# Pairing gate's last whole block with the block of the 64 last features, and seven block products in place of eight

## The chip, the cores and the metric

The kernel runs on one core of one Trainium2 chip. The metric is the device time of one execution in microseconds (us), lower is better. Times of single instructions come from the hardware profile of one execution.

## The reference

All arrays are float32. Only the second half of the computation, the feed-forward part, is touched by the change.

```python
# x: 2048 rows of 1024 values; F = 2752 features
x = x + layernorm(attention(layernorm(x)))
xt = layernorm(x)
up   = xt @ W_up.T            # W_up, W_gate: [2752, 1024]
gate = silu(xt @ W_gate.T)
y = gate * up @ W_down.T      # W_down: [1024, 2752]
out = x + layernorm(y)
```

The 2752 features are 21 whole blocks of 128 and one block of 64.

## The kernel before

**Precision.** A float32 operand is held as two rounded parts, high and low. One multiplication is then three matmuls (high by high, high by low, low by high), issued by `mmc` (lines 601 to 606). Splitting an operand is one ScalarE cast (line 108) and one VectorE subtraction (line 109).

**Halves and quadrants.** The feed-forward part goes over the 2048 rows in two halves, `s` = 0 and 1, of two groups of 512 rows each. Within a half, xt's transpose is seen as a 2 by 2 arrangement: B11 and B21 are the first and second 512 inputs of the first row group, B22 belongs to the second group. T1 to T4 are sums of these quadrants, built once a half.

**Products.** `prod(o, w, a, b)` multiplies a quadrant of 128 features by 512 inputs with one of B11, B21, B22, T1 to T4 of 512 inputs by 512 rows: four blocks of the inputs by three matmuls, 12 matmuls of 128x128 weights on 128x512 moving data, summed in one PSUM bank.

**Ten pairs.** For twenty of the feature blocks, block `p` and block `p + 10` are the two rows of a 2 by 2 quadrant matrix (class `Pair`, from line 493). The four quadrant results of such a matrix, which would take eight products, take seven: A11 by B11, A12 by B21, S1 by T1, S2 by T2, S3 by T3, A22 by T4, S4 by B22. S1 to S4 are sums of weight quadrants, made on VectorE by four operations of 128x512 (lines 528 to 531). `gate_up` (line 622) does this for gate and for up in turn, one product of gate and one of up, in the four banks `ag`, `au`, `cg`, `cu`.

**The rest.** What is left over is gate's block 20, up's block 20 and `wlast`, which holds the 64 last features of gate and the 64 last of up. Each is a `Single`: four products, A11 by B11 copied from bank `a` to SBUF and used again for the second row group, A11 by T1 and A12 by B22 in bank `c`, A12 by B21 added onto bank `a`. `gate_up_rest` (line 692) does the three of them, 12 products a half. Its results go to DRAM as `hr_d` (the whole block) and `hl_d` (the 64 features), each for row group 0 and 1.

**Down.** `run_down` follows with 78 steps a half, each a matmul of hidden features with W_down. It works in the other four banks.

**Buffers.** Weights pass through two rings. A load (512 KB from the SyncE queue) takes a raw buffer, of which there are four. A preparation (cast and subtraction, after the sums where there are some) takes one of six slots. A slot comes free when the last product that reads it is done (`done()`), and then the `Feeder` starts the next loads and preparations in a fixed order. A `Pair` takes two raw buffers and four slots, a `Single` and a step of down one raw buffer and one slot.

**Order.** Each engine's order is not the order of the text: a planner (`schedule_with_timeline_sim=True`) simulates the program when it is built. When an engine is free in that simulation, it gives it the instruction that is earliest in the text among those that are ready. So an engine that would wait is handed later work that is ready; the order so found is fixed in the kernel that runs. Where `keep_in_program_order` is used, the text's order holds.

Of the kernel before, what the change touches and what calls it, by code (L numbers as in the profile page):

```python
# [11 lines left out]
ALU = mybir.AluOpType  # L12
# [3 lines left out]
P = 128  # L16
# [10 lines left out]
FR = F - FB * P  # L27
NKB = T // P
EPS = 1e-5
NPAIR = 10  # L30
# [4 lines left out]
def block_kernel(ctx, tc, x, wqk, wv, bqk, bv, wo, bo, wgu, wlast, wd, out):  # L35
# [12 lines left out]
    nc = tc.nc  # L48
# [4 lines left out]
    def tl(p, shape, dt, name):  # L53
        return p.tile(shape, dt, tag=name, name=name, bufs=1)
# [32 lines left out]
    hl_d = [[tl(dram, [FR, 512], F32, f"hl_d{s}_{k}") for k in range(2)] for s in range(2)]  # L87
# [281 lines left out]
    def xq(name, cb):  # L369
        if name == "T2":  # L370
            return q2[cb // 2][:, cb % 2, :, :]
        t, c = XQ[name]
        return t[:, c + cb, :, :]
# [45 lines left out]
    class First:  # L419


        def __init__(self, dst, halves):
            self.dst, self.halves = dst, halves

        def load(self, r):
            self.r = r
            for h, d in zip((L, R), self.halves):
                nc.sync.dma_start(r[:, h], d)
# [58 lines left out]
    def w4(t):  # L487
        return t.rearrange("p (c h f) -> p c h f", h=2, f=P)
# [4 lines left out]
    class Pair:  # L493


        def __init__(self, p, m):
            self.p, self.m = p, m
            self.s = {}
            one, two_, three, four = Slot(), Slot(), Slot(), Slot()
            self.slot = [one, two_, three, four]  # L500

            self.at = {"A11": (one, 0), "A12": (one, 4), "S2": (two_, 0), "S1": (two_, 4), "S3": (three, 0), "S4": (three, 4), "A22": (four, 0)}
# [3 lines left out]

        def load(self):
            self.r = [raws.get(), raws.get()]
            for r, fb in zip(self.r, (self.p, self.p + NPAIR)):
                nc.sync.dma_start(r.rearrange("p (c f) -> p c f", f=P), wgu[fb, self.m])  # L510
            self.loaded = True

        loaded = False
# [87 lines left out]
    def mmc(o, w, m, first, last, chained, pin=lambda m: m):  # L601

        for n, (i, j) in enumerate(((0, 0), (0, 1), (1, 0))):
            one = nc.tensor.matmul(o, w[i], m[j], start=first and n == 0, stop=last and n == 2, skip_group_check=chained)  # L604
            if n == 0:
                pin(one)

    def prod(o, w, a, b, first=True):

        slot, c0 = w.at[a]  # L610
        v = w4(slot.need())
        for cb in range(4):
            x = xq(b, cb)
            mmc(o, (v[:, c0 + cb, 0, :], v[:, c0 + cb, 1, :]), (x[:, 0, :], x[:, 1, :]), first and cb == 0, cb == 3, not first)

    def add(o, a, b, op=ALU.add):
        nc.vector.tensor_tensor(o, a, b, op)  # L617

    def silu(o, a):
        nc.scalar.activation(o, a, AF.Silu)  # L620
# [68 lines left out]
        put("S2", u11)  # L689
        put("S4", g12)  # L690

    def gate_up_rest(s, wg, wu, wl, bg):
        ag, au, cg, cu = bg
        g11, g12, g22, g21, u11, u12, u22 = tmp[0:7]
        for w, a, c, u in ((wg, ag, cg, g12), (wu, au, cu, u12)):
            prod(a, w, "A11", "B11")
            nc.scalar.copy(u, a)
            prod(c, w, "A11", "T1")
        for w, a, c in ((wg, ag, cg), (wu, au, cu)):
            prod(a, w, "A12", "B21", False)  # L700
            prod(c, w, "A12", "B22", False)
            w.one.done()
        silu(g11, ag)
        add(g11, au, g11, ALU.mult)
        nc.sync.dma_start(hr_d[s][0], g11)
        add(g12, cg, g12)
        silu(g12, g12)
        add(u12, cu, u12)
        add(g12, g12, u12, ALU.mult)
        nc.sync.dma_start(hr_d[s][1], g12)  # L710
        prod(ag, wl, "A11", "B11")
        nc.scalar.copy(u11, ag)
        prod(cg, wl, "A11", "T1")
        prod(ag, wl, "A12", "B21", False)
        prod(cg, wl, "A12", "B22", False)
        wl.one.done()
        silu(g21[:FR, :], ag[:FR, :])
        add(g21[:FR, :], ag[FR : 2 * FR, :], g21[:FR, :], ALU.mult)
        nc.sync.dma_start(hl_d[s][0], g21[:FR, :])
        add(g22[:FR, :], cg[:FR, :], u11[:FR, :])  # L720
        silu(g22[:FR, :], g22[:FR, :])
        add(u22[:FR, :], cg[FR : 2 * FR, :], u11[FR : 2 * FR, :])
        add(g22[:FR, :], g22[:FR, :], u22[:FR, :], ALU.mult)
        nc.sync.dma_start(hl_d[s][1], g22[:FR, :])

    def load_down(p):
        for r, fb in zip(f4[0:2], (p, p + NPAIR)):
# [136 lines left out]
    X, Y = bank[0:4], bank[4:8]  # L864
    half = []
    for s in range(2):
        pairs = [(Pair(p, 0), Pair(p, 1)) for p in range(NPAIR)]
        rest = Single(wgu[2 * NPAIR, 0]), Single(wgu[2 * NPAIR, 1]), Single(wlast)
        dn = Down(s)
        half.append((pairs, rest, dn))  # L870
        for wg, wu in pairs:
            wg.queue_load()
            wu.queue_load()
            for i in range(4):
                wg.queue_prep(i)
                wu.queue_prep(i)
        for w in rest:
            w.queue_load()
            w.queue_prep(0)
        dn.queue()  # L880


# [85 lines left out]
    for s in range(2):  # L968
        pairs, rest, dn = half[s]
        bg, other = (X, Y) if s == 0 else (Y, X)  # L970
        for p in range(NPAIR):
            jobs = [] if s else [lambda: ahead(p), lambda: behind(p)]
            gate_up(s, p, *pairs[p], bg, jobs)
        gate_up_rest(s, *rest, bg)

        def next_x(cb):
            r1, r2 = raws2.get(), raws2.get()
            build_x(2, cb, r1, r2)
            raws2.free(r1)
            raws2.free(r2)  # L980

        if s == 0:
            run_down(s, dn, other, bg, 2 * TB * [None], [lambda cb=cb: next_x(cb) for cb in range(4)])
        else:
            xpool.release()
            x1pool = pool("x1", side="right")
            x1 = [tl(x1pool, [P, C], F32, f"x1_{k}") for k in range(2 * TB)]
            run_down(s, dn, other, bg, x1, [lambda k=k: nc.sync.dma_start(x1[k], x1_d[2 * TB + k]) for k in range(2 * TB)])
# [39 lines left out]
```

## Time and profile before

| | us |
|---|---|
| median of 3 runs | 1729.71 |
| lowest and highest | 1728.43 and 1729.87 |
| the profiled execution, its own time | 1728.61 |
| its span, first to last instruction | 1726.8 |
| TensorE busy | 1699.3 |
| VectorE busy | 1091.8 |
| ScalarE busy | 689.1 |

The granted TensorE clock was 0.992 of full in the mean. In the profile, PE is TensorE's matmuls, PEld its weight loads, DVE VectorE, ACT ScalarE, POOL GpSimd, SP SyncE. A group of instructions is written as line, engine, operation, output<-inputs by the program's names without their numbers: `xi` are the tiles for results (`g11`, `u12` and so on), `bank` the PSUM banks. A weight slot lies in `a` or in `wvo`; the quadrants of x are `xb` (B11, B21), `kx` (T1, T3), `qa` and `qb` (T2), `a` (T4, B22). So `bank<-xb,a` is a product with B11 or B21, `bank<-kx,a` one with T1 or T3, and `bank<-a` or `bank<-wvo` alone a step of down, whose two operands share a slot.

### The profile page before, as it was taken

The numbers are of one execution on the slowest core, as the hardware profiler recorded it, in microseconds if no ns is written. First come the engines' busy times: TensorE is split into PE (matmuls) and PEld (weight loads), VectorE is DVE, ScalarE is ACT, GpSimd is POOL, SyncE is SP. The second block draws the span as 40 slices with busy tenths as digits, with TensorE's granted clock in tenths as the row PEclk, the third lists the DMA queues.
The fourth block names the chain that finished last, engine by engine and source line by source line (L and its number), as shares of the span: only waits on it lengthen the run. The fifth ranks groups of instructions, "written<-read, shape, count | busy, mean of one in ns | idle before, by whom it ended". The sixth has DMA issues, their size and how long they took to land.

```text
span 1726.8 us, 21119 instructions
## 1 busy us (share of the span) xinstructions
PE 1699.3 (98%) x7788; PEld 1393.6 (81%) x7788; DVE 1091.8 (63%) x1666; ACT 689.1 (40%) x1031; POOL 89.0 (5%) x118
## 2 busy tenths in 40 slices
PE   8999999999899999999999999999999999999997
PEld 7888887888688888888888888788888888888886
DVE  8633667667877777676378457866555564345458
ACT  3222445544544444443355444433333333244343
POOL 1000001000011111110000000100000000000001
PEclk8999999999899999999999999999999999999999
DMA  6221023234755566665358655633332223486654
GB/s 210 80 80 37 37 74 125 97 126 172 257 195 195 201 215 214 214 204 190 122 191 255 194 194 193 205 105 113 129 109 94 91 92 122 132 280 195 195 185 159
DMA packets 131015, 271.01 MB, mean 157 GB/s; under 512 B 13280, under 2 KB 29792, under 8 KB 130912
## 3 DMA queue, kind: packets, MB, share of 16 engines
q1 hardware_dynamic: 128176, 262.72, 45.6%
q10 hardware_dynamic: 2736, 6.95, 1.1%
q8 instruction: 61, 1.00, 0.2%
q14 instruction: 42, 0.34, 0.1%
HBM read 185.73 MB, written 83.89 MB: 156 GB/s over the span
## 4 chain that ended last, share of the span: by engine, by line
PE 93%; DVE 3%; DMA 2%; issue 1%; ACT 1%; POOL 0%; SPq 0%; POOLq 0%; DVEq 0%; ACTq 0%
PE bank L604 70%; PE bank L146 4%; PE bank L145 4%; PE bank L147 4%; PE bank L275 3%; PE bank L276 2%; PE bank L267 1%; PE bank L205 1%; PE bank L206 1%; PE bank L346 1%; DMA f<-x 1%; PE bank L138 1%; DVE small L115 0%; PE bank L773 0%; PE bank L774 0%
## 5 line engine op out<-in xcount | busy, mean ns | idle before, releaser
L604 PE MATMUL bank<-a 128*128 128x512 f32 x1176 | 273.8, 390 | 0.0
L604 PEld LDWEIGHTS bank<-a 128*128 128x128 f32 x1176 | 220.8, 188 | 46.8
L604 PE MATMUL bank<-xb,a 128*128 128x512 f32 x816 | 197.3, 395 | 0.0
L109 DVE TENSOR_TENSOR a<-f2p,a 128x1024 fp32r<-128x1024 f32 (+2 forms) x114 | 124.7, 1095 | 93.4 <-ACT a L108 81.0
L617 DVE TENSOR_TENSOR xi<-bank,xi 128x512 f32<-128x512 f32 (+1 forms) x168 | 113.3, 685 | 111.1 <-PE bank L604 70.1
L604 PEld LDWEIGHTS bank<-xb,a 128*128 128x128 f32 x816 | 152.9, 187 | 37.1
L604 PE MATMUL bank<-kx,a 128*128 128x512 f32 x648 | 157.1, 395 | 0.0
L604 PE MATMUL bank<-a,a 128*128 128x512 f32 x648 | 153.4, 390 | 0.0
L108 ACT CAST a<-f2p 128x1024 fp32r<-128x1024 f32 (+2 forms) x114 | 107.6, 949 | 112.5 <-PE bank L604 102.4
L109 DVE TENSOR_TENSOR a<-f,a 128x512 fp32r<-128x512 f32 (+3 forms) x93 | 91.3, 981 | 91.4 <-ACT a L108 88.0
L604 PEld LDWEIGHTS bank<-kx,a 128*128 128x128 f32 x648 | 121.5, 187 | 29.5
L604 PEld LDWEIGHTS bank<-a,a 128*128 128x128 f32 x648 | 121.6, 188 | 26.4
L604 PE MATMUL bank<-wvo 128*128 128x512 f32 x600 | 142.4, 390 | 0.0
L604 PEld LDWEIGHTS bank<-wvo 128*128 128x128 f32 x600 | 112.6, 188 | 24.4
L108 ACT CAST a<-f 128x512 fp32r<-128x512 f32 (+3 forms) x93 | 69.4, 747 | 125.7 <-PE bank L604 90.6
L275 PE MATMUL bank<-a,a 128*128 128x512 f32 x256 | 94.5, 402 | 2.8 <-ACT f L348 2.0
L109 DVE TENSOR_TENSOR wvo<-f2p,wvo 128x1024 fp32r<-128x1024 f32 (+2 forms) x48 | 54.8, 1141 | 66.2 <-ACT wvo L108 57.6
L604 PE MATMUL bank<-a,wvo 128*128 128x512 f32 x384 | 93.7, 396 | 1.2 <-ACT xi L663 1.2
L604 PE MATMUL bank<-kx,wvo 128*128 128x512 f32 x384 | 91.9, 390 | 0.0
L617 DVE TENSOR_TENSOR xi<-xi,xi 128x512 f32<-128x512 f32 x124 | 85.4, 688 | 4.3
L604 PEld LDWEIGHTS bank<-a,wvo 128*128 128x128 f32 x384 | 72.0, 188 | 18.8 <-ACT xi L663 1.6
L604 PEld LDWEIGHTS bank<-kx,wvo 128*128 128x128 f32 x384 | 72.1, 188 | 15.7
(234 smaller groups left out, 2751.2 us busy)
## 6 DMA issues: line engine op xcount, KB each, us to landing
f2p<-wgu SPq DMA_DIRECT2D x43, 512.0 KB, 5.0
hd_S<-xi SPq DMA_DIRECT2D x80, 256.0 KB, 4.6
f<-x SPq DMA_DIRECT2D x30, 512.0 KB, 3.9
hd_A<-xi SPq DMA_DIRECT2D x60, 256.0 KB, 2.0
f<-wgu SPq DMA_DIRECT2D x21, 512.0 KB, 4.4
wr<-wgu SPq DMA_DIRECT2D x20, 512.0 KB, 5.9
f<-wd SPq DMA_DIRECT2D x20, 512.0 KB, 5.0
td_T<-f SPq DMA_DIRECT2D x40, 256.0 KB, 4.5
```

What stands on the lines that cost most here:

```text
L108: nc.scalar.copy(hi, src)
L109: (lo_engine or nc.vector).tensor_tensor(lo, src, f32(hi), ALU.subtract)
L138: nc.tensor.transpose(b[:, j * P : (j + 1) * P], t[:, cb * P : (cb + 1) * P], ident)
L145: nc.tensor.matmul(o, w[0], m[0], start=first, stop=False)
L146: nc.tensor.matmul(o, w[0], m[1], start=False, stop=False)
L147: nc.tensor.matmul(o, w[1], m[0], start=False, stop=last)
L205: nc.tensor.matmul(b, xg[:, c, 0, cols], wv_s[:, c, :, :].rearrange("p a f -> p (a f)"), start=(c == 0), stop=False)
L206: nc.tensor.matmul(b[:, D:], xg[:, c, 1, cols], wv_s[:, c, 0, :], start=False, stop=(c == 7))
L275: nc.tensor.matmul(b, p[:, k, 0, :], vt[:, k, :, :].rearrange("p h d -> p (h d)"), start=(k == 0), stop=False)
L276: nc.tensor.matmul(b[:, D:], p[:, k, 1, :], vt[:, k, 0, :], start=False, stop=(k == NKB - 1))
L604: one = nc.tensor.matmul(o, w[i], m[j], start=first and n == 0, stop=last and n == 2, skip_group_check=chained)
L617: nc.vector.tensor_tensor(o, a, b, op)
```

## The change

Gate's block 20 and `wlast` become the two rows of one `Pair`, with the seven products. Up's block 20 stays a `Single` with four. Its products are placed among the first eight. A half's `gate_up_rest` has 11 products where it had 12. The weights of the rest are prepared in the order: the pair's A11 and A12, up's, then the pair's S2 and S1, its S3 and S4, its A22. `Pair` takes its two sources as arguments.

```diff
-        def __init__(self, p, m):
-            self.p, self.m = p, m
+        def __init__(self, *src):
+            self.src = src
...
-            for r, fb in zip(self.r, (self.p, self.p + NPAIR)):
-                nc.sync.dma_start(r.rearrange("p (c f) -> p c f", f=P), wgu[fb, self.m])
+            for r, w in zip(self.r, self.src):
+                nc.sync.dma_start(r.rearrange("p (c f) -> p c f", f=P), w)
...
-    def gate_up_rest(s, wg, wu, wl, bg):
-        ag, au, cg, cu = bg
+    def gate_up_rest(s, wp, wu, bg):
+        ap, au, cp, cu = bg
         g11, g12, g22, g21, u11, u12, u22 = tmp[0:7]
-        for w, a, c, u in ((wg, ag, cg, g12), (wu, au, cu, u12)):
-            prod(a, w, "A11", "B11")
-            nc.scalar.copy(u, a)
-            prod(c, w, "A11", "T1")
-        for w, a, c in ((wg, ag, cg), (wu, au, cu)):
-            prod(a, w, "A12", "B21", False)
-            prod(c, w, "A12", "B22", False)
-            w.one.done()
-        silu(g11, ag)
+        prod(ap, wp, "A11", "B11")
+        nc.scalar.copy(g11, ap)
+        prod(au, wu, "A11", "B11")
+        nc.scalar.copy(u12, au)
+        prod(cp, wp, "A12", "B21")
+        wp.slot[0].done()
+        add(g11, cp, g11)
+        silu(g11, g11)
+        prod(cu, wu, "A11", "T1")
+        prod(ap, wp, "S2", "T2", False)
+        nc.scalar.copy(g12, ap)
+        prod(au, wu, "A12", "B21", False)
         add(g11, au, g11, ALU.mult)
         nc.sync.dma_start(hr_d[s][0], g11)
-        add(g12, cg, g12)
+        prod(cp, wp, "S1", "T1")
+        wp.slot[1].done()
+        prod(cu, wu, "A12", "B22", False)
+        wu.one.done()
+        add(u12, cu, u12)
+        prod(ap, wp, "S3", "T3", False)
+        nc.scalar.copy(g22, ap)
+        add(u22[:FR, :], cp[FR : 2 * FR, :], g22[FR : 2 * FR, :])
+        add(g22[:FR, :], cp[:FR, :], g22[:FR, :])
+        silu(g22[:FR, :], g22[:FR, :])
+        add(g22[:FR, :], g22[:FR, :], u22[:FR, :], ALU.mult)
+        nc.sync.dma_start(hl_d[s][1], g22[:FR, :])
+        prod(ap, wp, "A22", "T4", False)
+        wp.slot[3].done()
+        silu(g21[:FR, :], ap[:FR, :])
+        add(g21[:FR, :], ap[FR : 2 * FR, :], g21[:FR, :], ALU.mult)
+        nc.sync.dma_start(hl_d[s][0], g21[:FR, :])
+        prod(cp, wp, "S4", "B22", False)
+        wp.slot[2].done()
+        add(g12, cp, g12)
         silu(g12, g12)
-        add(u12, cu, u12)
         add(g12, g12, u12, ALU.mult)
         nc.sync.dma_start(hr_d[s][1], g12)
-        prod(ag, wl, "A11", "B11")
-        nc.scalar.copy(u11, ag)
-        prod(cg, wl, "A11", "T1")
-        prod(ag, wl, "A12", "B21", False)
-        prod(cg, wl, "A12", "B22", False)
-        wl.one.done()
-        silu(g21[:FR, :], ag[:FR, :])
-        add(g21[:FR, :], ag[FR : 2 * FR, :], g21[:FR, :], ALU.mult)
-        nc.sync.dma_start(hl_d[s][0], g21[:FR, :])
-        add(g22[:FR, :], cg[:FR, :], u11[:FR, :])
-        silu(g22[:FR, :], g22[:FR, :])
-        add(u22[:FR, :], cg[FR : 2 * FR, :], u11[FR : 2 * FR, :])
-        add(g22[:FR, :], g22[:FR, :], u22[:FR, :], ALU.mult)
-        nc.sync.dma_start(hl_d[s][1], g22[:FR, :])
...
-        pairs = [(Pair(p, 0), Pair(p, 1)) for p in range(NPAIR)]
-        rest = Single(wgu[2 * NPAIR, 0]), Single(wgu[2 * NPAIR, 1]), Single(wlast)
+        pairs = [tuple(Pair(wgu[p, m], wgu[p + NPAIR, m]) for m in range(2)) for p in range(NPAIR)]
+        rest = Pair(wgu[2 * NPAIR, 0], wlast), Single(wgu[2 * NPAIR, 1])
...
         for w in rest:
             w.queue_load()
-            w.queue_prep(0)
+        wp, wu = rest
+        wp.queue_prep(0)
+        wu.queue_prep(0)
+        for i in range(1, 4):
+            wp.queue_prep(i)
         dn.queue()
```

## The prediction

> **What bounds the kernel now.** I read the page's busy shares first, then the chain of work that ended last, then the stages by time, and last the two places where `gate_up_rest` runs.
>
> ```profile
> span 1726.8 us, 21119 instructions
> PE 1699.3 (98%) x7788; PEld 1393.6 (81%) x7788; DVE 1091.8 (63%) x1666; ACT 689.1 (40%) x1031; POOL 89.0 (5%) x118
> PE 93%; DVE 3%; DMA 2%; issue 1%; ACT 1%; POOL 0%; SPq 0%; POOLq 0%; DVEq 0%; ACTq 0%
> 775.07 157.52 PE bank L604 x684
> ```
>
> TensorE is the bound. The last line is a piece of the chain: 684 matmuls follow each other for 157.52 us, 230 ns each, with nothing in between; the first `gate_up_rest` lies inside this piece. The stages by time, where the first number is the stage, then its length, then busy time and instructions of PE, PEld, DVE and ACT, confirm it for both places:
>
> ```profile
> 841.57:875.50 33.93, 33.93 (x147) 27.38 (x146) 13.90 (x18) 8.62 (x12) 0.00 (x0) 1.00 0.36 127
> 1474.31:1507.94 33.63, 33.63 (x147) 27.40 (x146) 10.69 (x15) 6.93 (x10) 0.00 (x0) 1.00 0.38 129
> ```
>
> TensorE has no idle time in them at full clock; DVE is busy 41% and 32%, ACT 25% and 21%, the DMA engines 36% and 38%. A matmul fewer here is time gained, unless a wait takes its place. Such waits are, at present, covered by other work, as the timeline of TensorE shows (start, length, engine, line, operation, output<-inputs, count):
>
> ```profile
> 844.37 0.63 PE L604 MATMUL bank<-a 128*128 128x512 f32 x2
> ...
> 875.50 2.46 PE L604 MATMUL bank<-a 128*128 128x512 f32 x10
> ```
>
> `bank<-a` is a step of down. Two of the first step's 12 matmuls were taken by the planner from behind the rest, more than 130 matmuls later in the text, and set between the rest's first and second product; the other ten follow when the rest is over. The second half has the same two at 1477.11.
>
> **What the Trainium skill says.** "Perfetto Trace Analysis", section Identifying the Most-Contended Engine, warns that matmul busy time is a poor measure of nearness to the roofline and asks for the weight loads' share. The trace agrees that the two differ, 98% and 81%; that TensorE is the bound rests here on the spacing and the chain. "TensorE: Matmul & The Clock Gate", section Back-to-back issue gap, gives about 216 ns for an isolated matmul of 512 columns and about 131 ns sustained. The trace has 230 ns in a stream with a weight load each, so I use that. The same page, section Step-by-step, says that matmuls stay in program order and only weight loads are pulled ahead: a matmul that waits for a bank holds all behind it. Its section Architectural detail says that ScalarE and VectorE are strict queues: a copy out of a bank waits behind a cast put before it. The trace shows both in one place, where no later work was left to fill in:
>
> ```profile
> 1118.33 3.02 PE L604 MATMUL bank<-xb,wvo 128*128 128x512 f32 x12 [0.24 <-ACT xi L620]
> ...
> 1121.37 0.62 ACT L108 CAST wvo<-f 128x512 fp32r<-128x512 f32 x1 [3.10 <-DVE f L529]
> 1121.90 0.58 ACT L663 COPY xi<-bank 128x512 f32<-128x512 f32 x1
> ...
> 1122.53 3.06 PE L604 MATMUL bank<-a,wvo 128*128 128x512 f32 x12 [1.19 <-ACT xi L663]
> ```
>
> A product ends at about 1121.35, its copy waits behind a cast, and the next product in that bank begins 1.19 us late.
>
> **The change, part by part.**
>
> Matmuls. One product of 12 goes in each half, 24 in all. The two stages hold 146 matmuls each (144 of the rest and the two of down): 33.93 / 146 = 0.2324 us and 33.63 / 146 = 0.2303 us. 12 x 0.2324 + 12 x 0.2303 = **5.55 us** saved, on the path.
>
> The new tail. Up's four products are over after the eighth, so S3 by T3 and A22 by T4 follow each other in bank `ap`, with a copy to `g22` between. Every other copy or read of a bank has at least one product, 2.78 us, between it and the next write. Uncovered, this wait costs the copy, 0.59 us, and about 0.1 us around it, so 0.7 us; with a cast of 128x1024 in front (1.05 us) 1.75 us. That is 1.4 to 3.5 us for both halves. Queued behind A22 by T4 on TensorE are S4 by B22 and all of down. The other end is nought: down's first step is ready at that point (its slot is prepared when the last pair ends), and the planner takes it as it did at 844.37. Only the error of its times is left. I take 0.3 us a half, **0.6 us** lost; nothing here can gain. S4 by B22 needs `cp` read twice by DVE (2 x 0.69) after the copy: some 2.2 us with the copy, behind 2.78 us of A22 by T4.
>
> Preparations. A `Pair` makes five casts and five subtractions where two `Single`s made two of each, and four sums. By columns, subtraction: before 2 x 1.22, now 2 x 1.22 + 3 x 0.69, so 2.1 more; sums 4 x 0.69 = 2.8; one more reading of a bank, 0.7: DVE 5.6 us a half more. ACT: 3 x 0.62 for casts and 0.59 for one copy more, 2.5 us. They fall into the last pair and the rest; DVE's gap of 11.7 us from 847.3 to 859.05 and ACT's 8.3 us gap cover them. Were the cover gone, the pair's S2 would come late; it is needed at the fifth product, some 20 us after the slot for it is free. I take nothing. A gain is excluded, since none of it stood on the path.
>
> Slots. The rest uses five where it used three. Followed through the rings, the first step of down is prepared when the last pair ends (before: the third), and the next five after the rest's products 3, 7, 8, 10 and 11 (before, after 6, 8 and 12 for the last three). At down's start both have the same six steps. The sixth is freed at the rest's end and is needed five steps of 2.75 us later, 13.7 us; cast and subtraction take 2.3. Nothing.
>
> Transfers. Three loads of 512 KB and four stores a half, as before. `hl_d` and the second `hr_d` leave in the last products' wake instead of the first `hr_d` pair in the middle; SP's queue carries down's loads behind them, by at most the wait for one result. Landing takes 2.4 to 3.5 us and down's reads come ten steps later or more. `u12`'s copy waits for an earlier store of that tile as line 697 does now (till 851.1); its bank is written again only at product 6, after 855. Nothing.
>
> Knock-on. Each order after the rest is planned anew. The two waits at 1118 and 1122, 0.24 + 1.19 = 1.43 us, may go or double: 1.4 us to either side, 0 taken.
>
> Sum: 1728.61 - 5.55 + 0.6 = 1723.66 us for the profiled execution (span 1726.8 - 4.95 = 1721.85). The median of the runs stood 1.10 us above that execution: **1724.8 us**.
>
> **The rivals.**
>
> *The wait is not filled* (0.20). For: at 1122.53 a copy after a cast did stop TensorE. Against: there the text had no ready work left. Here it has. Gain 5.55 less 1.4 to 3.5, so 1725.6 to 1727.7, in the middle 1726.6.
>
> *Slower, by late weights* (0.08). The sums, casts and stores of the new pair hold DVE, ACT or SP behind a wait, and the S quadrants or down's first steps reach their slots late. Each half must then lose over 4.5 us, (5.55 + 3.46) / 2, where 3.46 us is 0.2% of the time; a late load costs its landing, 5.9 us in the slowest row of such weights, with 1.05 + 1.22 us of preparation: 8.2 us a half, 1729.7 - 5.6 + 16.4 = 1740.5. Against: lead times of 13 to 20 us found above.
>
> *Nothing is gained* because a product removed were work that only filled a wait (0.06): TensorE would stand idle somewhere before down. The chain shows no such wait; it would be 1729.7, at most 1731.
>
> **How the numbers follow.** The main case has 0.66: 1724.8, and 1722.3 to 1726.8 with no wait at all, a better or worse order at the second half's start and 0.5 us of spread. The range for 8 in 10 adds the unfilled waits: 1721.8 to 1728.6. About 0.2%, 3.46 us, is what a measurement of this kernel tells from no change; the line is 1726.25. Of the main case 0.60 lies below it and 0.06 above; of the unfilled waits 0.08 below; the rest of these and of the idle case, 0.18, within; with 0.08 slower.
>
> **What would show it.** In the profile after: 7764 matmuls; TensorE without a gap through both rests; each rest's own 132 matmuls in about 30.6 us; some matmuls `bank<-a` or `bank<-wvo` of down between S3 by T3 (`kx`) and A22 by T4. A wait of PE L604 for an ACT `xi` copy of 0.7 us or more in both halves shows the first rival; a wait for a cast or subtraction of line 108 or 109 the second. A TensorE busy without gaps and a time within 1 us of before would show the sum itself wrong.

## The result and the profile after

| | before | after |
|---|---|---|
| median of 13 runs each, us | 1728.43 | 1725.12 |
| lowest and highest | 1726.91 and 1729.87 | 1723.65 and 1727.36 |
| profiled execution, own time and span | 1728.61, 1726.8 | 1724.01, 1722.2 |

The ratio is 0.998 with a 95% interval of 0.9972 to 0.9987: faster by 3.3 us where 4.9 were forecast. The same kernel, run again with the experiments, gave 0.9983 (0.9977 to 0.999), 3.0 us. The time forecast, 1724.8, lies within 0.3 us of the median after, and that is luck: the three runs of before from which it was reckoned had a median 1.3 us above that of all 13, and the saving was forecast 1.6 us too large, so that two errors cancel.

The page of the changed kernel:

```profile
span 1722.2 us, 21102 instructions
PE 1694.8 (98%) x7764; PEld 1387.4 (81%) x7764; DVE 1101.3 (64%) x1682; ACT 693.4 (40%) x1039; POOL 89.0 (5%) x118
PE 96%; DVE 2%; issue 1%; DMA 1%; ACT 1%; POOL 0%; POOLq 0%; DVEq 0%; SPq 0%; ACTq 0%
```

There are 24 matmuls fewer. DVE is busy for 9.5 us more and ACT for 4.3 us more, and TensorE carries the chain as before. The stages of the two rests, in the form of the table of before:

```profile
841.29:877.01 35.72, 35.72 (x155) 28.89 (x154) 17.53 (x21) 12.08 (x15) 0.00 (x0) 1.00 0.38 130
1471.42:1507.06 35.64, 35.64 (x156) 28.89 (x154) 15.21 (x19) 10.28 (x13) 0.00 (x0) 1.00 0.63 234
```

TensorE has no idle time here either. Each stage holds 154 matmuls, 132 of the rest and 22 of down. Where those 22 stand is seen in the timeline of the first rest around the new tail, all engines:

```profile
865.73 0.86 PE L604 MATMUL bank<-kx,a 128*128 128x512 f32 x3
...
866.43 2.92 PE L604 MATMUL bank<-wvo 128*128 128x512 f32 x12
866.63 0.59 ACT L717 COPY xi<-bank 128x512 f32<-128x512 f32 x1 [3.12 <-PE bank L604]
867.25 1.39 DVE L617 TENSOR_TENSOR xi<-bank,xi 64x512 f32<-64x512 f32 x2 [1.54 <-ACT xi L717]
...
869.19 2.46 PE L604 MATMUL bank<-a 128*128 128x512 f32 x10
...
871.49 0.86 PE L604 MATMUL bank<-a,wvo 128*128 128x512 f32 x3
```

S3 by T3 (`kx`) ends, 22 matmuls of down run from 866.43 to 871.49, and the copy and both readings of `cp` are over by 868.7. A22 by T4 (`a,wvo`) begins without a wait. So the saving on the path is whole up to here, and what is missing must have gone elsewhere. The chain of waits names the stages. First before, then after, pieces of matmuls with nothing between them (start, length, line, count):

```profile
934.43 112.01 PE bank L604 x492
...
1122.53 442.47 PE bank L604 x1920
1566.82 112.02 PE bank L604 x492
```

```profile
931.53 112.51 PE bank L604 x492
...
1561.59 112.49 PE bank L604 x492
```

Down's 492 matmuls are the same work, and take 0.50 and 0.47 us longer after the change, with no gap. The matmuls themselves are spaced wider.

### The profile page after: what moved, and what is told of

The parts are those of the page before. It is cut to its first block, busy times and chain, and to the rows that moved or that the text cites. A ratio compares the mean times of both kernels' runs of the same rounds, so it can differ in the third digit from the quotient of the medians.

```text
span 1722.2 us, 21102 instructions
## 1 busy us (share of the span) xinstructions
PE 1694.8 (98%) x7764; PEld 1387.4 (81%) x7764; DVE 1101.3 (64%) x1682; ACT 693.4 (40%) x1039; POOL 89.0 (5%) x118
## 4 chain that ended last, share of the span: by engine, by line
PE 96%; DVE 2%; issue 1%; DMA 1%; ACT 1%; POOL 0%; POOLq 0%; DVEq 0%; SPq 0%; ACTq 0%
PE bank L604 72%; PE bank L146 4%; PE bank L145 4%; PE bank L147 4%; PE bank L275 3%; PE bank L276 2%; PE bank L205 1%; PE bank L267 1%; PE bank L206 1%; PE bank L346 1%; PE bank L138 1%; DVE small L115 0%; PE bank L782 0%; PE bank L783 0%; DMA f<-xT_d 0%
## 5 line engine op out<-in xcount | busy, mean ns | idle before, releaser
L604 PE MATMUL bank<-xb,a 128*128 128x512 f32 x912 | 218.1, 395 | 0.0
L604 PEld LDWEIGHTS bank<-xb,a 128*128 128x128 f32 x912 | 170.9, 187 | 41.6
L109 DVE TENSOR_TENSOR a<-f,a 128x1024 fp32r<-128x1024 f32 (+2 forms) x91 | 91.3, 1003 | 116.7 <-ACT a L108 103.1
L604 PE MATMUL bank<-a,a 128*128 128x512 f32 x588 | 141.0, 391 | 0.0
L604 PEld LDWEIGHTS bank<-a,a 128*128 128x128 f32 x588 | 110.4, 188 | 24.3
L108 ACT CAST a<-f 128x1024 fp32r<-128x1024 f32 (+2 forms) x91 | 69.4, 763 | 146.4 <-PE bank L604 115.8
L604 PE MATMUL bank<-a,wvo 128*128 128x512 f32 x444 | 109.0, 395 | 0.0
L604 PEld LDWEIGHTS bank<-a,wvo 128*128 128x128 f32 x444 | 83.4, 188 | 19.9
L109 DVE TENSOR_TENSOR wvo<-f,wvo 128x1024 fp32r<-128x1024 f32 (+1 forms) x52 | 60.8, 1169 | 58.8 <-ACT wvo L108 58.7
L275 PE MATMUL bank<-a,a 128*128 128x512 f32 x256 | 94.5, 402 | 2.8 <-ACT f L348 2.0
L617 DVE TENSOR_TENSOR xi<-xi,xi 128x512 f32<-128x512 f32 (+1 forms) x124 | 85.3, 688 | 5.7 <-ACT xi L620 1.5
```

The costliest lines, as they stand in the source:

```text
L108: nc.scalar.copy(hi, src)
L109: (lo_engine or nc.vector).tensor_tensor(lo, src, f32(hi), ALU.subtract)
L275: nc.tensor.matmul(b, p[:, k, 0, :], vt[:, k, :, :].rearrange("p h d -> p (h d)"), start=(k == 0), stop=False)
```

## The spacing of matmuls, and what was tested

I measured from each matmul's start to the next one's, over the whole feed-forward part (transposes left out, anything above 300 ns taken as a wait and counted as 230), and sorted the intervals by where the two operands lie that TensorE reads at the same time: the moving data of one matmul, and the weights of the next. The compiled program places the tiles at these addresses of a partition: `a1`, `a2` at 10 to 75 KB (thousand bytes), `qb` at 114 to 123, and `xb`, `kx`, `wvo`, `qa` at 139 to 229. Call the first three low and the others high. In the trace of before the next weights begin to load 3 ns after a matmul's start, so the two are indeed read together. "TensorE: Matmul & The Clock Gate" in the Trainium skill, section Step-by-step, has two separate read ports for moving data and weights, so that loading the next weights takes no reading bandwidth from the running matmul. This trace shows a small dependence on where the two lie, and does not show its reason:

| kernel before | intervals | mean |
|---|---|---|
| both low or both high | 3362 | 227.5 ns |
| one low, one high | 2146 | 233.3 ns |

The two kinds can be seen by eye in the timeline of the changed kernel, in three products of 12 matmuls in the second half:

```profile
1474.17 2.95 PE L604 MATMUL bank<-xb,a 128*128 128x512 f32 x12
1476.96 2.89 PE L604 MATMUL bank<-xb,wvo 128*128 128x512 f32 x12
1479.69 2.96 PE L604 MATMUL bank<-kx,a 128*128 128x512 f32 x12
1482.49 1.56 PE L604 MATMUL bank<-qa,a 128*128 128x512 f32 x6
```

From one start to the next: 2.79 us with weights in `a2`, 2.73 with weights in `wvo`, 2.80 with `a2` again.

Neither tile is slow by itself. In the second half's pairs of the kernel before, the moving data of `kx` and of `a1` (the first `a` of `a,a`, and the `a` of `a,wvo`) meet weights in both places. The number before the last bar is the mean length of one matmul in ns:

```profile
L604 PE MATMUL bank<-kx,a 128*128 128x512 f32 x310 | 75.3, 395 | 0.0
L604 PE MATMUL bank<-a,a 128*128 128x512 f32 x288 | 67.5, 390 | 0.0
...
L604 PE MATMUL bank<-kx,wvo 128*128 128x512 f32 x108 | 26.8, 391 | 0.0
L604 PE MATMUL bank<-a,wvo 128*128 128x512 f32 x96 | 23.7, 395 | 0.0
```

`kx` is slower with weights in `a2`, `a1` with weights in `wvo`. The ends of matmuls are modelled, but the starts over the whole feed-forward part say the same: with `kx`, 233.3 ns to the next start beside `a2` and 227.9 beside `wvo`; with `a1`, 227.8 and 233.1. The recorded weight load is as long in both kinds, 187.7 ns on the same side and 187.6 on different ones.

The slots of the ring are four in `a2` and two in `wvo`, and a preparation takes whichever came free first. The new rest takes five slots and returns them in another order, so everything that follows stands in other places. Three theories were put to the runs. **Count**: a matmul removed is worth its 231 ns and all else is covered. **Place**: besides that, the slots' new places cost time. **Order**: the planner's new order moves the waits at the start of the second half.

Each kernel ran beside the kernel before on the same chip (before: 1727.92 us for the first four, 1728.65 for the next four, 1728.45 for the last three).

**e1_drop: the 24 matmuls alone.** This is the kernel before with one of up's products left out in each half.

```diff
             prod(a, w, "A12", "B21", False)
-            prod(c, w, "A12", "B22", False)
+            if w is wg:
+                prod(c, w, "A12", "B22", False)
```

> The kernel before without up's product A12 by B22 in both halves: 24 matmuls fewer, nothing else edited (up's second row group lacks that term). Count theory (a removed matmul is worth its 231 ns, all else is covered): 5.55 us below before, ratio 0.9968. Place theory (on top of that, a matmul takes about 6 ns more when its moving data and the next matmul's weights lie on different sides of SBUF): 2136 such meetings against 2146 before, so the same 5.6 us; the changed kernel has 2353 and therefore gained less. Cover theory (a removed product only uncovers waits): less than 3 us.

Measured: 1722.37 us, 5.55 below, ratio 0.9972 (0.9962 to 0.9982). Removing 24 matmuls without moving a slot is worth the whole price worked out for them. The first term of the prediction's sum stands, and the changed kernel falls short of it by some 2.3 us.

**e2_nofill: the wait uncovered.** The first matmul of each bank in down's first five steps is kept in program order.

```diff
...
-                mm_step(banks[t], steps[i], t, first and i == 0, i == len(steps) - 1, not first)
+                mm_step(banks[t], steps[i], t, first and i == 0, i == len(steps) - 1, not first, pin if i < hold else (lambda m: m))
...
```

> The changed kernel with the first five steps of down held behind the rest in the text's order, so nothing can be set between S3 by T3 and A22 by T4. If the fill hid the wait: TensorE stops twice for the copy to g22, 0.7 to 1.75 us each, 1.4 to 3.5 us above the changed kernel, ratio to before about 0.9990 to 1.0. If the fill was idle decoration, because the wait is shorter than the profile's numbers say: within 0.5 us of the changed kernel.

Measured: 1727.44 us, ratio 0.9995 (0.9987 to 1.0003), so 2.5 to 2.8 us of the saving are gone by the medians, with an uncertainty of more than 1 us. The timeline of this kernel at the place:

```profile
864.82 2.97 PE L604 MATMUL bank<-kx,a 128*128 128x512 f32 x12
...
867.82 0.59 ACT L717 COPY xi<-bank 128x512 f32<-128x512 f32 x1 [3.12 <-PE bank L604]
...
868.46 3.06 PE L604 MATMUL bank<-a,wvo 128*128 128x512 f32 x12 [0.68 <-ACT xi L717]
```

TensorE waits 0.68 us for the copy. By starts, the last matmul of S3 by T3 to the first of A22 by T4 took 1073 ns and the next interval 338, where 233 is usual: 0.95 us lost, and the same in the second half, 1.9 us together. The fill hides that. It lies in the lower part of the 1.4 to 3.5 us that the prediction gave, since no cast stood in front of the copy; but such a bare wait costs 0.95 us a half, where the prediction had 0.7.

**e3_between: another cover.**

```diff
-        prod(cu, wu, "A12", "B22", False)
-        wu.one.done()
-        add(u12, cu, u12)
         prod(ap, wp, "S3", "T3", False)
         nc.scalar.copy(g22, ap)
+        prod(cu, wu, "A12", "B22", False)
+        wu.one.done()
+        add(u12, cu, u12)
```

> The changed kernel with up's product A12 by B22 moved in the text to between S3 by T3 and A22 by T4. The wait then has a product of 2.78 us before it without any fill. If the fill costs nothing: the same time as the changed kernel within 0.7 us. If setting steps of down among the products costs something (22 of its matmuls stand there in each half): faster than the changed kernel by more than that.

Measured: 1725.35 us, ratio 0.9986 (0.9979 to 0.9992), 2.6 us below before; the two runs of the changed kernel gave 3.3 and 3.0. The planner still set some of down's matmuls behind the product moved there, 10 in each half (in the first from 866.39 to 868.68), so the run compares 10 with 22 and not none with 22. Between these, filling costs nothing that shows.

**e4_half2 and e5_half1: one half at a time.** Both versions of the rest stand in the kernel, and the half decides.

```diff
...
-        gate_up_rest(s, *rest, bg)
+        (gate_up_rest if s == 1 else gate_up_three)(s, *rest, bg)
```

> The change in the second half alone; the first half keeps the three blocks with twelve products. Count theory: 12 matmuls, 2.77 us below before. Place theory: 2137 meetings against 2146, so the same 2.8 us here, and only 1.5 us when the first half alone is changed, because the ring of slots is permuted there and the second half's pairs take the worse places. Order theory (each new plan moves the waits at the start of the second half, 1.43 us in the profile of before): the 1.43 us stay here, since all before the second rest is unchanged.

> The change in the first half alone. Count theory: 2.77 us below before, as for the second half alone. Place theory: 12 matmuls less 2.77 us, but 2353 meetings of moving data and weights on different sides against 2146, 207 x 6 ns = 1.24 us more: 1.5 us below before; in the profile the second half's pairs take longer and the first half's do not. Order theory: the waits of 1.43 us at the start of the second half may be gone, then 2.9 us below.

Measured: the second half alone 1725.71 us, 2.2 below, ratio 0.9986 (0.998 to 0.9993). The first half alone 1728.5 us, 0.15 below, ratio 1.0002 (0.9993 to 1.001). The second half's pairs and rest, from the chain of waits of e4_half2, of e5_half1, and of the changed kernel's second profile (e9_after_again):

```profile
1123.36 439.67 PE bank L604 x1908
```

```profile
1120.74 444.01 PE bank L604 x1920
```

```profile
1121.33 441.25 PE bank L604 x1908
```

Before, it was 442.47 us for 1920. In e4_half2, 12 matmuls fewer took 2.80 us less, 233 ns each. In e5_half1, where this stretch of code is as before and only the first half's rest was changed, the same 1920 matmuls took 1.54 us more. The changed kernel has both: 1.22 us less. Only place had foretold this: for e5_half1, count had said 2.8 us below before and order 2.9. Place had undersized the loss, with 1.5 us below by expectation and 0.15 as measured: a widening in down of the same kind as above came on top.

**e6_order132 and e10_order132_again: the ring's order in down.**

```diff
-        for i in range(1, 4):
+        for i in (1, 3, 2):
             wp.queue_prep(i)
```

> The changed kernel with the pair's A22 prepared before its S3 and S4, which leaves the two wvo slots next to each other in the ring during down, as before the change. Place theory: 2271 meetings against 2353, 82 x 6 ns, 0.5 us below the changed kernel, found in down's stages (492 matmuls in 112.0 us as before, not 112.5). Count theory: no change in any stage.

> The changed kernel with A22 prepared before S3 and S4, once more beside the changed kernel. Its earlier profile had the matmuls' spacing 2.6 us shorter in sum (2271 meetings, and fewer slow matmuls next to a change of slot in down): 2.6 us below the changed kernel. Count theory: no difference.

Measured: 1723.3 us, ratio 0.9971 (0.9959 to 0.9982), and again 1722.37 us, ratio 0.9966 (0.9954 to 0.9978). The changed kernel beside it, **e9_after_again**, took 1725.42 us (0.9983, 0.9977 to 0.999).

> The changed kernel itself, as the measure for the two others on the same chip: 0.998 of before, some 3.4 us below it, 2353 meetings of moving data and weights on different sides.

So one line that only swaps two preparations is worth 3.0 us by these two medians, 2.4 of them in the spacing of matmuls (the table below). The forecasts for it were 0.5 us and then 2.6. Its chain of waits (e10_order132_again) gives down back the old lengths:

```profile
931.32 112.05 PE bank L604 x492
...
1560.30 112.03 PE bank L604 x492
```

The timelines of TensorE at the beginning of the first of these stretches show what differs, first in the changed kernel, then in e10_order132_again, where the last line ends with the window asked for:

```profile
931.37 2.92 PE L604 MATMUL bank<-wvo 128*128 128x512 f32 x12
934.12 2.92 PE L604 MATMUL bank<-a 128*128 128x512 f32 x12
936.87 2.92 PE L604 MATMUL bank<-wvo 128*128 128x512 f32 x12
939.63 8.35 PE L604 MATMUL bank<-a 128*128 128x512 f32 x36
```

```profile
931.16 2.89 PE L604 MATMUL bank<-a 128*128 128x512 f32 x12
933.88 5.63 PE L604 MATMUL bank<-wvo 128*128 128x512 f32 x24
939.36 5.85 PE L604 MATMUL bank<-a 128*128 128x512 f32 x25
```

A step takes both operands from one slot, so sides meet only where the slot changes, four times in six steps after the change and twice with the swapped order. Each change costs more than its one wide interval of 235 ns. Within a slot the intervals settle at 226.7 ns, but the first six after a change to `a2` have 231 and 230 ns, and the first nine after a change to `wvo` 228, 232 and 228, in means of three. That is some 23 and 26 ns beside the 8 of the change itself, and this is what the expectation of 0.5 us for e6_order132 lacked. Where one slot follows another on the same side, no such widening is seen.

**e7_sides_best and e8_sides_worst: places chosen.** A slot is taken by side in place of in turn; (0,) puts the pairs' A11 and A12 into `wvo` (and up's last block with them), (3,) the pairs' A22.

```diff
...
+        IN_WVO = (0,)
...
-                slot.t = slots.get()
+                slot.t = slots.get(self.slot.index(slot) in self.IN_WVO)
...
```

> The changed kernel with slots chosen by place: a pair's A11 and A12, which meet B11 and B21 in xb, go into wvo on the same side, all other weights of pairs into a2, on the side of a1 (T4, B22). Same work, same instructions. Place theory: 1523 meetings against 2353, 830 x 6 ns = 5.0 us below the changed kernel, about 1720, ratio to before 0.995. Count theory: the same time as the changed kernel, or slower where a slot is waited for.

> As the kernel with slots chosen by place, but with A22 (which meets T4 in a1) in wvo and all other weights of pairs in a2: 2859 meetings against 2353. Place theory: 506 x 6 ns = 3.0 us above the changed kernel, about 1728. Count theory: the same as the changed kernel. A cost of the choice itself (slots waited for) would show here and in the other choice with the same sign.

Measured: the worst choice 1728.52 us, ratio 1.0 (0.9991 to 1.0008), about 3 us above the changed kernel, as place foretold. The best choice 1729.71 us, ratio 1.0007 (1.0 to 1.0014), some 4 us above the changed kernel where 5 below were expected. As a choice for the time it failed, and by the time alone it would fit count, which allowed for slots that are waited for. Its waits say why (engine, line, waited for, us in total, times, longest):

```profile
PE bank L617 <- DVE xi L630: 3.5, 5, 0.9
PE bank L617 <- ACT xi L672: 3.1, 2, 2.9
```

One longer wait, of 7.1 us, stands at the start of the feed-forward part; it ends at 455.6 us, as that of the changed kernel does in its two profiles (454.4 and 455.8). The waits of these two lines all lie in the first half's pairs, where the extra work of residuals and of W_down's sums also runs, and where the changed kernel has no such wait. In one of them the cast of a weight stood at the head of ACT's queue and waited 6.58 us for its load, with the copy out of a bank behind it:

```profile
674.12 1.05 ACT L108 CAST wvo<-f2p 128x1024 fp32r<-128x1024 f32 x1 [6.58 <-DMA f2p<-wgu]
...
675.07 0.58 ACT L672 COPY xi<-bank 128x512 f32<-128x512 f32 x1
```

Waits after 470 us, beyond those that every kernel has there, add up to 9.4 us by starts. The spacing itself did narrow, by 5.5 us against the changed kernel, and this is what speaks for place. The likely reason for the late load, which no run isolates, is in the edit: a preparation that must have a certain slot comes later, and its raw buffer is free for the next load only then.

**e11_second_half_placed: both findings together.** The swapped order, and places chosen in the second half alone, where ACT and DVE have more room.

```diff
...
+        for w in sum(pairs, ()) + rest:
+            w.fifo = s == 0
...
-        for i in range(1, 4):
+        for i in (1, 3, 2):
             wp.queue_prep(i)
...
```

> The same, and in the second half alone the pairs' A11 and A12 in wvo and their other weights in a2; the first half takes slots in turn, as VectorE is busier there and slots chosen by place were waited for. Place theory: 1955 meetings against 2271, 316 x 6 ns = 1.9 us below the kernel with the changed order, 4.5 us below the changed kernel, about 1720.5 where before takes 1728.5. If the choice of slots is waited for here too (13 us of waits when both halves chose): slower than the changed kernel, with waits of TensorE for ACT or DVE in the second half's pairs.

Measured: 1721.92 us, ratio 0.9963 (0.9951 to 0.9975), the lowest median of all, 3.5 us below the changed kernel, where 4.5 were expected, and 6.5 below before. Beside e10_order132_again it is 0.45 us lower where 1.9 were expected, which the intervals don't tell from nothing; in the profile its second half is narrower as foretold, 473.47 us against 475.89 for the same 2060 matmuls.

**All kernels against one sum.** The second column is the sum of all intervals by the method above, waits left out, against before (1265.7 us); the third what waits of the kind that the edit made add; the last the medians' difference.

| kernel | intervals, us | waits, us | measured, us |
|---|---|---|---|
| changed | -2.3 | 0 | -3.3, -3.0 |
| e1_drop | -5.5 | 0 | -5.6 |
| e2_nofill | -2.4 | +1.9 | -0.5 |
| e3_between | -2.3 | 0 | -2.6 |
| e4_half2 | -2.8 | 0 | -2.2 |
| e5_half1 | +0.4 | 0 | -0.2 |
| e6 and e10, order | -4.9, -4.7 | 0 | -5.4, -6.1 |
| e8_sides_worst | -0.1 | 0 | -0.1 |
| e7_sides_best | -7.8 | +9.4 | +1.1 |
| e11_second_half_placed | -6.8 | 0 | -6.5 |

No row is off by more than 1.4 us. That much is in the waits at the start of the second half, which come and go between executions of one program: the changed kernel's first profile has none there, its second this one:

```profile
PE bank L604 <- ACT xi L663: 1.1, 1, 1.1
```

## Why the prediction was right, and where it was not

- **The bound and the price of a matmul: right.** 24 matmuls were worth 5.55 us by the sum and 5.55 by e1_drop.
- **The new tail: right in its mechanism.** The planner filled the gap; 0.6 us had been set aside for its errors, and none was lost, since 22 matmuls cover 5.1 us where an uncovered wait takes 0.95. The rival of the unfilled wait is real (e2_nofill), but was not what happened.
- **Preparations: right.** DVE took 9.5 us more and ACT 4.3, where 11.2 and 5.0 were worked out, and no wait of TensorE came of it.
- **Slots: the step that failed.** "Nothing" was right of the supply: no step of down came late. It was wrong of the places. The prediction followed which slot each step takes and did not ask where the slot lies. That term measures 5.5 - 2.3 = 3.2 us: 1.5 us in the second half's pairs and rest, 1.0 us in the two stretches of down shown, and the rest in the shorter pieces. The sum should have read 5.55 - 3.2 - 0 = 2.3 us, to which the waits of the second half add what they happen to give. By the medians the saving is 3.3 and 3.0 us, so the missed term is 2.3 to 2.5 us; what the medians give beyond the spacing is put down to these waits, but no run holds them still.
- **Knock-on: left open rightly, taken wrongly as the plan's.** Waits of this kind were nought in one execution of the changed kernel and some 1.6 us in another, so a new plan is not needed to move them.
- **Chances.** A time shorter by over 0.2% had 0.68. The measured ratios, 0.998 and 0.9983, stand at that line or short of it; had the places been counted, that case would have been given less.

Two of the signs named beforehand were seen: 7764 matmuls, and down's matmuls between `kx` and T4. The third, rests "in about 30.6 us" for their own 132 matmuls, holds too: less the 5.06 and 5.05 us of down's 22, 35.72 and 35.64 us leave 30.7 and 30.6. None of them could show the loss, which lay after the rest.

## What to carry to other kernels

Where matmuls follow each other without gaps, count them, and then ask of each whether its moving data and the next one's weights lie on the same side: in this kernel some 6 ns of 230, with the slow matmuls after each change, took 2.3 us (by the medians) to 3.2 us (by the spacing) of a saving of 5.5. An edit that takes a different number of buffers from a ring moves every later user of it, so compare stretches of code that the edit did not touch. Choose the places through the order in which buffers are returned, which added no wait here, before forcing them, which did.

## What the runs showed of the hardware

- The spacing of 128x512 matmuls with a new weight load each, in this kernel: 226.7 ns settled in one slot, 233.3 ns in the mean where moving data and next weights lie on different sides, the same in every run (233.3 to 233.5 in thirteen profiles).
- After a change of side in down it takes five intervals (into `a2`) or seven (into `wvo`) to come back to 226.7 ns.
- What makes a side is not settled: no tile of weights lay between 75 and 205 KB, `qb` (114 to 123) behaved in between (231 ns with weights in `a2`, 233 to 234 in `wvo`), and intervals of one kind still differ among themselves (231 to 235 ns with `kx` and `a2`). That the addresses and not something else that goes with a slot are the cause is supported by the crossing of `kx` and `a1` above and by the choice of places moving the spacing both ways (5.5 us narrower and 2.2 us wider than the changed kernel), and by no run that moves a tile alone; that was not tried.
